# Moving steps between the slots of a scan: u one slot up, x_proj and softplus two slots apart, part of the MLP and the next norm behind softplus

## The chip, the cores and the metric

The kernel runs on one core of one Trainium2 chip. The metric is the device time of one execution in microseconds (us). Three runs of the kernel before gave 12441.65 us as the median, with 12438.44 and 12444.25 us at the ends.

## The reference

The network has four layers over an image `x` of 4 x 256 x 64 x 64 (batch, channels, rows, columns), each of the form `x = x + layer(groupnorm(x))`. Layers 0 and 1 are a gated recurrence followed by window attention. Layer 2 is a Mamba layer over the 4096 tokens of an image with 512 inner channels. Layer 3 is a grouped Mamba layer: the 256 channels are cut into 4 groups of 64, each group has 128 inner channels, and all groups share the weights. The change touches layers 2 and 3. Both have this core, and layer 3 has an MLP and an output convolution after it:

```
xi, z  = split(xn @ in_proj)                    # xn: layer norm of the tokens
u      = silu(causal_conv4(xi) + conv_b)
dt, B, C = split(u @ x_proj)
delta  = softplus(dt @ dt_proj + dt_b)
h_t    = exp(delta_t * A) * h_(t-1) + (delta_t * u_t) * B_t     # 16 states a channel
y      = (sum_n h_n * C_n + u * D) * silu(z)
layer 2:  out = y @ out_proj
layer 3:  m = layernorm(y @ out_proj)
          m = gelu(m @ fc1 + b1) @ fc2 + b2 + skip * xn
          out = silu(batchnorm(outc @ m))
```

## The kernel before

`net_kernel` loops over the 4 images of the batch and runs the attention layers, `mamba_layer` and `grouped_mamba_layer` on each. Nothing overlaps between images except at the edges, so the program is four nearly equal pieces.

**Slots.** Both Mamba layers hand a list of 16 blocks to `scan_blocks`: 4 chunks `k` of 1024 tokens by 4 blocks of 128 channels. A block has 16 slots, one for each state `n`. In layer 3 a block is one channel group; the four groups of a chunk form two pairs `c = 0, 1`, and a pair is an *even* block followed by an *odd* one. So the blocks of a chunk are even c=0, odd c=0, even c=1, odd c=1.

**What a slot issues.** The order is written out by hand (manual schedule), and each engine executes its instructions in that order. For slot `i`, `scan_blocks` issues, in this order: on VectorE (DVE) the product `pb = du * B` (L914) and the scan `h` (L920); on GpSimd (POOL) `product(i + 2)` (L830) and `hc = h * C` (L926); on ScalarE (ACT) `decay(i + 3)`, which is `da = exp(delta * A)` (L856), and `keep` of the last column (L861); the loads of C and B rows on the DMA queue; then the background steps of the slot, `blk["bg"]`; then on TensorE (PE) `spread(i + 2)`, which broadcasts a row of B into PSUM (L844), and `turn(i - 1)`, eight transposes that sum `hc` into `y` (L872); and last `decay(i + 2, True)` on ACT.

**Slots apart.** Slots 0, 4 and 8 of layer 3 (0, 5 and 10 of layer 2) are *apart*: their product with B is made on POOL from a loaded row (`bb`), so DVE has no L914 there and PE no spread. Their decay is the tile `dap`, written to PSUM, and it is issued at the end of the slot two before, behind that slot's background steps:

```
            for step in blk["bg"].get(n, ()):
                step()
            ...
            spread(i + 2)
            turn(i - 1)
            decay(i + 2, True)
```

**Buffers.** `da` has four buffers, `h` and `hc` three, the PSUM tiles `pb` and `dap` share two, and all other PSUM work of a layer shares two buffers of the tag `mm`.

**Background steps.** `put(block, slots, steps)` hangs steps on slots. The ones that the change moves are these.

- `all_u` / `in_u` (L1574, L1581): the four convolution taps as matmuls, four pieces of a pair; the first of two pieces takes both `mm` buffers, the second evicts them on ACT. `silu(.., "u")` (L1606) loads an activation table, takes Silu of the two tiles and loads the exp/ln table back (L950).
- `x_proj` (`table_steps`): two projections evicted on ACT (L1073), the second with the stores of B and C to DRAM; then a copy to bf16 on ACT (`part(P)`, L1081), a POOL difference (`rest(64)`, L1084), an ACT copy (`part(64)`) and a POOL difference (`rest(32)`), which give the three bf16 parts that spread reads.
- `delta` (`delta_steps`, "softplus"): `proj(s)` is a matmul and Abs, Exp, Ln on ACT (L1043 to L1045), `add(s)` is a DVE step (L1049), `times_u` a POOL product (L1053).
- `mlp`: `out_proj` (L1642, two ACT steps L1647 and L1648), `deviation` (L1652, then Ln and Exp), `scale` (POOL, L1657), `hidden(0)` (L1663), `fc1` (table load, Gelu, `hidden(1)` on PE, Gelu, table load; L1670), `fc2(0)`, `fc2(1)` (L1686, L1691, eviction L1696). `m0` and `m1` are the halves of the pair before.
- `norm` of the next chunk: `mean`, `center`, `deviation`, `scale`, `affine`; `h0` and `h1` are its halves. `out_conv` (L1711, L1717) is the output convolution, `out` (L1736) adds x on POOL and stores.

The product of `y` with `silu(z)` is two DVE steps of slot 3 (L886), which read the `mm` tiles `fin_ps` (L897) of slot 2.

Of the kernel before, what the change touches and what calls it, by code (L numbers as in the profile page):

```python
# [45 lines left out]
class Net:  # L46
# [1068 lines left out]
    def mamba_layer(self, x, bridge, pe_dram, w_in, w_cw, w_x, w_dt, w_out, v_dram):  # L1115
        tc, nc = self.tc, self.nc
        ND = 4
        with ExitStack() as ctx:
# [148 lines left out]
            def delta(k, d):  # L1267
                return self.delta_steps(
                    chunks[k]["blocks"][d], wdt[:, d * P : (d + 1) * P], work, psum
                )  # L1270
# [76 lines left out]
            for k in range(n_chunk):  # L1347
                more = k + 1 < n_chunk
                bg = [blk["bg"] for blk in chunks[k]["blocks"]]

                def put(d, where, steps):
                    for i, f in zip(where, steps):
                        bg[d].setdefault(i, []).append(f)

                if k == 0:
                    put(0, (2, 3, 4, 5), folds)
                if k:
                    for i, where in enumerate(((3, 4, 5), (6, 7, 8), (9, 10, 11), (12, 13, 14))):
                        put(0, where, out_proj(k - 1, i // 2, i % 2))
                put(0, (9, 10, 11, 12, 12), delta(k, 1))  # L1360
                put(0, (14, 15), (in_z(k, 0, 0), in_z(k, 0, 1)))
                put(1, (1,), (silu((k, 0, "zs")),))
                put(1, (6, 7, 8, 9, 10), delta(k, 2))
                put(1, (11, 12), (in_z(k, 1, 0), in_z(k, 1, 1)))
                put(1, (14,), (silu((k, 1, "zs")),))
                at = (6, 7, 8, 9, 10) if more else (5, 6, 7, 8, 9)
                put(2, at, delta(k, 3))
                at = (10, 11) if more else (8, 9)
                put(2, at, (in_z(k, 2, 0), in_z(k, 2, 1)))
                z3 = in_z(k, 3, 0), in_z(k, 3, 1)  # L1370
                if more:
                    put(3, (0, 1), z3)
                else:
                    put(2, (10, 11), z3)
                if more:

                    if k == 0:
                        put(0, (0,), (lambda: begin(1),))
                        put(0, (0, 0, 1, 3, 4, 5, 6, 7), self.later(lambda: norm(1, 0), 8))
                    h1 = self.later(lambda k=k: norm(k + 1, 1), 8)  # L1380
                    if k:
                        put(0, (2, 4, 5, 7, 8, 13, 14, 15), h1)
                    else:
                        put(0, (7, 8, 9, 12, 13, 14, 15), h1[:7])
                        put(1, (1,), h1[7:])
                    if k + 2 < n_chunk:
                        put(3, (3,), (lambda k=k: begin(k + 2),))
                        h0 = self.later(lambda k=k: norm(k + 2, 0), 8)
                        put(3, (4, 6, 7, 14, 15), h0[:5])
                        chunks[k + 1]["late"] = ((0, 1, 2), h0[5:])  # L1390
                    if k:
                        put(0, *chunks[k]["late"])
                    u = all_u(k + 1)
                    put(1, range(5, 16), u[:11])
                    put(2, range(14), u[11:25])
                    put(3, (1, 2, 3, 4, 5, 5, 6), u[25:])
                    xs = x_proj(k + 1)
                    put(2, (13,), (silu((k + 1, 0, "u"), (k + 1, 1, "u"), (k + 1, 2, "u"),
                                        (k, 2, "zs")),))
                    put(3, (7,), (silu((k + 1, 3, "u"), (k, 3, "zs")),))  # L1400
                    put(3, (7, 8, 8, 9, 9, 10, 11, 12), xs)
                    put(3, (9, 10, 10, 11, 12), delta(k + 1, 0))
                else:
                    put(2, (13,), (silu((k, 2, "zs"), (k, 3, "zs")),))

                    sums, about, square, squares, early_squares = stats

                    def square_into(i):
                        tag, bufs = ("pe", 1) if i % 2 else ("u", 5)
                        square(i, work.tile([P, NC], F32, tag=tag, name="cs_sq", bufs=bufs))  # L1410

                    for i in range(6):
                        put(1 + (13 + i) // DS, ((13 + i) % DS,), (lambda i=i: sums(i),))
                        put(2 + (12 + i) // DS, ((12 + i) % DS,), (lambda i=i: square_into(i),))
                        put(2 + (13 + i) // DS, ((13 + i) % DS,), (lambda i=i: squares(i),))
                    put(2, (3,), (about,))
                    put(3, (3,), (early_squares,))
                    for i in range(4):
                        at = (6 + 2 * i, 7 + 2 * i)
                        put(3, at, out_proj(k, i // 2, i % 2, ((0, 1, 2),)))  # L1420
# [70 lines left out]
    def grouped_mamba_layer(self, x, bridge, begun, ws_dram, outc_dram, v_dram, out_b):  # L1491
        tc, nc = self.tc, self.nc
        w_in, w_cw, w_x, w_dt, w_out, w_f1, w_f2 = ws_dram
        with ExitStack() as ctx:
# [113 lines left out]
            def silu(k, c, key, also=()):  # L1608
                def step():
                    for blk in chunks[k]["blocks"][2 * c : 2 * c + 2]:  # L1610
                        silu_of(blk, key)
                    for f in also:
                        f()
                    self.exp_ln_tables()

                return step
# [14 lines left out]
            def delta(k, q):  # L1631
                return self.delta_steps(chunks[k]["blocks"][q], wdt, work, psum)
# [108 lines left out]
            def all_u(k, c):  # L1741
                return [in_u(k, c, s, i) for s in range(2) for i in range(2)]
# [109 lines left out]
            for i, (k, c) in enumerate(pairs):  # L1852
                even, odd = chunks[k]["blocks"][2 * c : 2 * c + 2]

                def put(blk, where, steps):
                    for i, f in zip(where, steps):
                        blk["bg"].setdefault(i, []).append(f)


                for where, steps in late:  # L1860
                    put(even, where, steps)
                late = []
                more = c == 1 and k + 1 < n_chunk

                if more:
                    h0, h1 = (self.later(lambda k=k, s=s: norm(k + 1, s), 5) for s in range(2))
                    put(even, (0,), (lambda k=k: begin(k + 1),))
                    put(even, (0, 1, 4, 5, 6), h0)
                    put(even, (14, 15), h1)
                    put(odd, (1, 2, 3), h1[2:])  # L1870
                put(even, (4, 5, 6, 7, 8, 9), x_proj(k, 2 * c + 1))
                if i:
                    m0, m1 = mlp(*pairs[i - 1], 0), mlp(*pairs[i - 1], 1)
                    put(even, (5, 6, 7, 10, 11, 12, 13), m0)
                    put(even, (6, 7, 8), m1)
                    if c == 0:
                        put(even, (14, 15), m1[3:])
                        put(odd, (0, 1), m1[5:])
                    else:
                        put(odd, (15,), m1[3:])  # L1880
                        late.append(((0, 1, 1), m1[4:]))
                put(even, (7, 8, 8, 9, 10), delta(k, 2 * c + 1))
                also = [lambda k=k: out_silu(k - 1)] if c == 1 and k else []
                if i == 0:
                    put(even, (1, 2), [in_z(0, 0, s) for s in range(2)])
                    put(even, (1, 2), [lambda ss=ss: scale(1, ss, nc.gpsimd) for ss in first])
                    put(even, (3, 3), [lambda ss=ss: affine(1, ss) for ss in first])
                    also = [lambda blk=odd: silu_of(blk, "u")]
                put(even, (3,), (silu(k, c, "zs", also),))
                if c == 1 and k:  # L1890
                    put(even, (4, 4, 5, 5), [out(k - 1, *sm) for sm in outs])
                if c == 0 and k:
                    put(odd, (10, 12, 15), [out_conv(k - 1, *sm) for sm in outs[:3]])
                    late.append(((0,), [out_conv(k - 1, *outs[3])]))

                if i + 1 < len(pairs):
                    nk, ncol = pairs[i + 1]
                    put(odd, (4, 5, 6, 7), all_u(nk, ncol))
                    put(odd, (7,), (silu(nk, ncol, "u"),))
                    put(odd, (8, 8, 8, 9, 10, 11), x_proj(nk, 2 * ncol))  # L1900
                    put(odd, (9, 10, 10, 11, 12), delta(nk, 2 * ncol))
                    put(odd, (13, 14), [in_z(nk, ncol, s) for s in range(2)])
            self.scan_blocks(
                [blk for c in chunks for blk in c["blocks"]], loop, psum, psb, psy, (0, 4, 8),
# [125 lines left out]
```

## Time and profile before

| what | us |
|---|---|
| median of three runs | 12441.65 |
| profiled execution, its own time | 12439.35 |
| span of the profiled execution | 12437.6 |
| DVE busy | 10216.3 (82%) |
| PE busy | 10255.9 (82%) |
| POOL busy | 9018.9 (73%) |
| ACT busy | 7245.9 (58%) |
| scans of layer 2, image 1 (4188.1 to 5141.5) | 953.40 |
| scans of layer 3, image 1 (5195.7 to 6162.7) | 967.00 |
| scans of layer 3, images 0, 2, 3 | 968.50, 967.10, 969.10 |

All times are us from the span's start. The line numbers are those of the kernel before. An engine's busy time counts its own instructions; idle time in front of an instruction is put down to the instruction that released it. The time of an execution is 1.75 us longer than its span.

### The profile page before, as it was taken

How to read it: one execution, taken by the hardware profiler on the slowest of the kernel's cores; microseconds unless marked ns; L12 is line 12 of the kernel's file. 1: busy time of each engine (PE TensorE's matmuls, PEld its weight loads, DVE VectorE, ACT ScalarE, POOL GpSimd, SP SyncE). 2: the span in 40 equal slices, each digit the busy share in tenths (PEclk: the TensorE clock that was granted, in tenths of full speed). 3: DMA queues.
4: the chain of work that ended last, by engine and by line, in shares of the span. 5: the costliest groups of instructions: out<-in, count | busy, mean ns of one | idle time of the engine just before them, and what ended most of it. 6: DMA issues, size and time to landing. Idle time of an engine off the chain costs nothing. (4 is left out here: it accounts for less than half of the span.)

```text
span 12437.6 us, 159552 instructions
## 1 busy us (share of the span) xinstructions
PE 10255.9 (82%) x54592; PEld 6015.9 (48%) x54592; DVE 10216.3 (82%) x9130; ACT 7245.9 (58%) x13300; POOL 9018.9 (73%) x4634
## 2 busy tenths in 40 slices
PE   8987887787898788777789878877878987887777
PEld 4664544443466454444346645444434664544443
DVE  6777898897677799889767779988976777998897
ACT  4565554776466555477645655547754565554775
POOL 4666886887466688688746668868874666886887
PEclk9999998999899999899889999989988999998998
DMA  3343554454334455454433434545543343554454
GB/s 96 108 128 131 168 169 147 167 169 142 97 108 127 132 169 170 146 168 167 144 95 109 127 130 172 169 146 167 169 142 95 109 127 130 172 170 146 167 170 140
DMA packets 680299, 1773.54 MB, mean 143 GB/s; under 512 B 89120, under 2 KB 195120, under 8 KB 678464
## 3 DMA queue, kind: packets, MB, share of 16 engines
q1 hardware_dynamic: 679488, 1763.34, 43.7%
q8 instruction: 435, 7.13, 0.2%
q14 instruction: 376, 3.08, 0.1%
HBM read 1601.51 MB, written 94.37 MB: 136 GB/s over the span
## 5 line engine op out<-in xcount | busy, mean ns | idle before, releaser
L926 POOL TENSOR_TENSOR hc<-h,cb 128x1024 f32<-128x1024 f32 x2056 | 4814.1, 2350 | 988.2 <-DVE h L920 425.6
L920 DVE TENSOR_TENSOR_SCAN h<-da,m_state,pb 128x1024 f32<-128x1024 f32 x1248 | 2919.9, 2340 | 161.7 <-DVE pb L914 2.8
L872 PE MATMUL y<-ident,hc 128*128 128x128 f32 x16384 | 2371.0, 293 | 346.7 <-POOL hc L926 259.0
L872 PEld LDWEIGHTS y<-ident,hc 128*128 128x128 f32 x16384 | 2091.8, 152 | 1009.7 <-POOL hc L926 439.0
L914 DVE TENSOR_TENSOR pb<-du,pb 128x1024 f32<-128x1024 f32 x1672 | 2024.8, 1211 | 92.5 <-PE pb L844 89.3
L856 ACT ACTIVATE da<-delta,m_v 128x1024 f32<-128x1024 f32 x1672 | 1898.8, 1141 | 220.8 <-DVE h L920 204.0
L844 PE MATMUL pb<-m_parts,pick 128*128 128x512 bf16 x3312 | 1099.8, 417 | 872.2 <-DVE h L920 821.8
L502 ACT ACTIVATE pr<-sc,mn 128x256 f32<-128x256 f32 x2048 | 956.6, 478 | 770.8 <-PE pt_ps L528 551.2
L514 POOL TENSOR_TENSOR pr<-pr,sm 128x1024 f32<-128x1024 f32 x512 | 967.9, 1897 | 560.0 <-DVE sm L512 380.6
L844 PEld LDWEIGHTS <-pick 128*128 128x128 bf16 x3312 | 255.2, 101 | 1883.1 <-DVE h L920 1160.3
L920 DVE TENSOR_TENSOR_SCAN h<-da,pb 128x1024 f32<-128x1024 f32 x424 | 969.6, 2287 | 55.6 <-DVE pb L914 1.4
L830 POOL TENSOR_TENSOR bb<-du,bb 128x1024 f32<-128x1024 f32 x376 | 888.8, 2364 | 65.2 <-DMA bb<-m_cd 60.5
L491 DVE TENSOR_REDUCE mn<-sc 128x4 f32<-128x1024 f32 x512 | 609.6, 1219 | 244.9 <-PE sc L480 242.8
L920 DVE TENSOR_TENSOR_SCAN h<-dap,m_state,bb 128x1024 f32<-128x1024 f32 x288 | 672.0, 2333 | 76.2 <-ACT dap L856 63.4
L528 PE MATMUL pt_ps<-ident,pr 128*128 128x128 f32 x4096 | 571.6, 283 | 145.7 <-ACT pts L541 64.3
L208 PE MATMUL conv_ps<-att_y,att_wb 128*128 128x512 f32 x1536 | 688.8, 593 | 0.0
L856 ACT ACTIVATE dap<-delta,m_v 128x1024 f32<-128x1024 f32 x376 | 419.6, 1116 | 422.3 <-DVE h L920 298.2
L552 PE MATMUL ov_ps<-pts,kv 128*64 128x128 f32 x8192 | 583.6, 289 | 91.6 <-DVE vimg L565 75.6
L480 PE MATMUL sc<-kv,q 64*128 64x128 f32 x8192 | 573.0, 288 | 81.7 <-DMA kv<-kv_dram 68.0
L528 PEld LDWEIGHTS pt_ps<-ident,pr 128*128 128x128 f32 x4096 | 465.8, 144 | 315.4 <-issue 151.4
L480 PEld LDWEIGHTS sc<-kv,q 64*128 64x128 f32 x8192 | 515.8, 196 | 124.3 <-issue 56.1
L552 PEld LDWEIGHTS ov_ps<-pts,kv 128*64 128x64 f32 x8192 | 456.4, 141 | 217.2 <-DVE vimg L565 131.9
(270 smaller groups left out, 18063.0 us busy)
## 6 DMA issues: line engine op xcount, KB each, us to landing
cb<-m_cd SPq DMA_DIRECT2D x2048, 512.0 KB
kv<-kv_dram SPq DMA_DIRECT2D x2048, 128.0 KB
bb<-m_cd SPq DMA_DIRECT2D x376, 512.0 KB
q<-q SPq DMA_DIRECT2D x256, 256.0 KB
kv_dram<-kst SPq DMA_DIRECT2D x128, 256.0 KB
kv_dram<-vn SPq DMA_DIRECT2D x128, 256.0 KB
x<-in_x_dram SPq DMA_DIRECT2D x8, 2048.0 KB
m_pe<-in_pe_dram SPq DMA_DIRECT2D x32, 512.0 KB
```

The lines of the kernel that those rows point to most:

```text
L480: nc.tensor.matmul(sc[w][:, r, cq, :], qbuf[sj % 2][m][rows, b, 2 * a + w].rearrange("p h t -> p (h t)"), t[rows, :, k0 : k0 + 64], start= ...
L502: nc.scalar.activation(t[:, cq].rearrange("p j r t -> p r j t"), sc[w][:, :, cq, :].rearrange("p r (j t) -> p r j t", j=2), AF.Exp, bias=m ...
L514: nc.gpsimd.tensor_tensor(t, t, s.rearrange("p (a o) -> p a o", o=1).to_broadcast([P, 4, 256]), ALU.mult,)
L528: nc.tensor.transpose(pt[w][j][:, cq, :], t[:, cq, j].rearrange("p r t -> p (r t)"), self.ident,)
L552: nc.tensor.matmul(ov[i][b * 64 : b * 64 + 64, m, :, :, w, :], t[:, j, c0 : c0 + 64], pts[w][j][:, cq, :], start=(j == 0), stop=(j == 1),)
L830: nc.gpsimd.tensor_tensor(pb[i], slots[i][0]["du"], pb[i], ALU.mult)
L844: nc.tensor.matmul(pb[i][:, ss], self.pick[:, n : n + 1].to_broadcast([P, P]), blk["parts"][:, ss], start=True, stop=True,)
L856: nc.scalar.activation(da[i], blk["delta"], AF.Exp, scale=blk["a"](n))
L872: nc.tensor.matmul(blk["y"][:, ss], t[:, ss], self.ident, is_transpose=True, start=(n == 0 and ss.start % NT == 0), stop=(n == DS - 1 and ...
L914: nc.vector.tensor_tensor(pb[i], blk["du"], pb[i], ALU.mult)
L920: nc.vector.tensor_tensor_scan(h[i][:, ss], da[i][:, ss], pb[i][:, ss], state, ALU.mult, ALU.add)
L926: nc.gpsimd.tensor_tensor(hc[i][:, ss], h[i][:, ss], cb[i][:, ss], ALU.mult)
```

## The change

Only `put` calls are changed; every step stays, and no tile or buffer count changes. In layer 2, x_proj's projections and softplus of block 3 are put two slots apart and the bf16 splitting follows softplus. In layer 3, odd blocks issue u and its Silu one slot earlier (3 to 6), x_proj's projections at 8 and 9, softplus from 10 and the splitting at 10 to 13, and the output convolution at 13 to 15. Even blocks issue the projections at 4 and 5, softplus from 7 (c=0) or 8 (c=1), the splitting at 10 to 13, the first steps of `m1` behind softplus, `m0` one slot later for c=1, and the rest of `h0` at 13 to 15.

```diff
@@ mamba_layer
-                    put(3, (7, 8, 8, 9, 9, 10, 11, 12), xs)
-                    put(3, (9, 10, 10, 11, 12), delta(k + 1, 0))
+                    put(3, (7, 8, 8, 9), xs)
+                    put(3, (10, 11, 11, 12, 12), delta(k + 1, 0))
+                    put(3, (10, 11, 12, 13), xs[4:])
@@ grouped_mamba_layer
                 if more:
                     ...
-                    put(even, (0, 1, 4, 5, 6), h0)
+                    put(even, (0, 1, 13, 14, 15), h0)
                     put(even, (14, 15), h1)
                     put(odd, (1, 2, 3), h1[2:])
-                put(even, (4, 5, 6, 7, 8, 9), x_proj(k, 2 * c + 1))
+                xs, ds = x_proj(k, 2 * c + 1), delta(k, 2 * c + 1)
+                put(even, (4, 5), xs)
+                put(even, (8, 9, 9, 10, 10) if c else (7, 8, 8, 9, 9), ds)
+                put(even, (10, 11, 12, 13), xs[2:])
                 if i:
                     m0, m1 = mlp(*pairs[i - 1], 0), mlp(*pairs[i - 1], 1)
-                    put(even, (5, 6, 7, 10, 11, 12, 13), m0)
-                    put(even, (6, 7, 8), m1)
+                    put(even, (10, 11, 12) if c else (9, 10, 11), m1)
+                    put(even, (6, 7, 8, 11, 12, 13, 13) if c else (5, 6, 7, 10, 11, 12, 13), m0)
                     ...
-                put(even, (7, 8, 8, 9, 10), delta(k, 2 * c + 1))
                 ...
                 if c == 0 and k:
-                    put(odd, (10, 12, 15), [out_conv(k - 1, *sm) for sm in outs[:3]])
+                    put(odd, (13, 14, 15), [out_conv(k - 1, *sm) for sm in outs[:3]])
                     ...
                 if i + 1 < len(pairs):
                     nk, ncol = pairs[i + 1]
-                    put(odd, (4, 5, 6, 7), all_u(nk, ncol))
-                    put(odd, (7,), (silu(nk, ncol, "u"),))
-                    put(odd, (8, 8, 8, 9, 10, 11), x_proj(nk, 2 * ncol))
-                    put(odd, (9, 10, 10, 11, 12), delta(nk, 2 * ncol))
+                    put(odd, (3, 4, 5, 6), all_u(nk, ncol))
+                    put(odd, (6,), (silu(nk, ncol, "u"),))
+                    xs = x_proj(nk, 2 * ncol)
+                    put(odd, (8, 9), xs)
+                    put(odd, (10, 11, 11, 12, 12), delta(nk, 2 * ncol))
+                    put(odd, (10, 11, 12, 13), xs[2:])
                     put(odd, (13, 14), [in_z(nk, ncol, s) for s in range(2)])
```

## The prediction

> **What bounds the kernel now.** I first read the stages by windows, since the change touches only the Mamba layers: layer 3's scans take about 967 us of each image, and DVE is busy for 873 of them.
>
> ```profile
> core 0: us, PE busy (x) PEld busy (x) DVE busy (x) ACT busy (x) POOL busy (x), PEclk, DMA share, GB/s
> 5195.70:6162.70 967.00, 741.24 (x3474) 410.98 (x3472) 873.21 (x531) 658.40 (x952) 852.84 (x387) 0.90 0.50 169
> ```
>
> So DVE sets the pace, and what can be won or lost in this layer is its idle time. POOL, at 853 us, has little room. Next I read who DVE waits for in the same window (us in total, times, longest):
>
> ```profile
> DVE delta L1049 <- ACT delta L1045: 33.7, 20, 2.6
> DVE pb L914 <- PE pb L844: 15.3, 13, 4.5
> DVE h L920 <- ACT dap L856: 12.3, 4, 4.2
> DVE h L920 <- POOL bb L830: 1.3, 1, 1.3
> ```
>
> The other images give 34.0, 33.6 and 33.8 us for the first line and 13.1, 12.9 and 12.6 for the third. The first line is softplus: `add(s)` waits for Abs, Exp and Ln of its half. Taken block by block it is 17.6 us in the seven odd blocks, 5.9 in the even c=0 and 10.1 in the even c=1 blocks. The third line is the even c=1 blocks alone.
>
> The timeline of ACT in an odd block (k=1, c=0) shows why softplus is late. Scan 6 starts at 5520.93, scan 7 at 5524.54, scan 8 at 5526.80, and scan 10 at 5533.98:
>
> ```profile
> 5521.28 1.15 ACT L856 ACTIVATE da<-delta,m_v 128x1024 f32<-128x1024 f32 x1
> ...
> 5523.32 1.12 ACT L856 ACTIVATE dap<-delta,m_v 128x1024 f32<-128x1024 f32 x1 [0.80 <-DVE h L920]
> ...
> 5526.39 1.27 ACT L1581 ACTIVATE m_u<-u_ps,m_v 128x512 f32<-128x512 f32 x2 [0.79 <-PE u_ps L1574]
> 5527.68 1.28 ACT L1606 ACT_TABLE_LOAD   x1
> 5528.97 2.00 ACT L1606 ACTIVATE m_u<-m_u 128x1024 f32<-128x1024 f32 x2
> 5530.98 1.28 ACT L950 ACT_TABLE_LOAD   x1
> ```
>
> Evictions, two loads and two Silu hold ACT from 5526.39 to 5532.26, 5.87 us, and all that follows is late until add(0) has waited 2.41 us. But `dap`, the decay of apart slot 8, stands ahead of this stretch, because Silu is in slot 7 and `dap` was issued at the end of slot 6. PE decides when the stretch can start:
>
> ```profile
> 5514.77 1.99 PE L1574 MATMUL u_ps<-m_xn,m_wi 64*128 64x512 f32 x8
> ...
> 5518.10 1.99 PE L1574 MATMUL u_ps<-m_xn,m_wi 64*128 64x512 f32 x8
> ...
> 5521.43 1.99 PE L1574 MATMUL u_ps<-m_xn,m_wi 64*128 64x512 f32 x8
> ...
> 5524.38 1.99 PE L1574 MATMUL u_ps<-m_xn,m_wi 64*128 64x512 f32 x8
> ```
>
> A piece of u with the spread and the transposes behind it takes 3.33 us of a slot of 3.60: here PE runs without a pause.
>
> **Odd blocks.** Softplus moves to slots 10 to 12, two slots behind x_proj, when ACT has caught up: its waits, 17.6 us an image, go. The Silu moves to slot 6, and the order of instructions puts it ahead of `dap` of slot 8. The wait added is DVE's scan 8 on `dap`; behind `dap` on ACT stand the decays of slots 10 and 11, and behind scan 8 hc of slot 8 on POOL and spread(10) on PE, none of which is late by itself. Its length: the first piece, now in slot 3, needs both `mm` buffers, which the slot's two products by silu(z) release at 5513.8 (DVE rows 5512.55, 1.26 long). That is 1.0 us before the old start, not 3.6, since PE had no pause to fill. Three periods of 3.33 later the fourth piece starts at 5523.8 and ends at 5525.8. ACT then needs 5.87 us and `dap` 1.12, with 0.1 for hand-over: 5532.9. Scan 8 could start 2.26 after scan 7. Scan 7 slips by 0.35, because spread(5) now stands behind the first piece (5513.8 + 2.0 + 0.5 = 5516.3 against 5515.99), so it could start at 5527.15. The wait is 5.8. New per image: 7 x (5.8 + 0.35) = 43.1; removed 17.6; together +25.5. Bounds of the wait: 3.6, if the slot-6 piece ran where the old slot-6 piece ran (ends 5523.4), and 6.6, if u were no earlier at all and PE 0.4 later, as it is in the c=1 blocks. I take 5.8 as it follows from consecutive rows.
>
> The Trainium skill, "ScalarE: Activation LUTs", section "Table sets: the hidden batching unit", charges about 2.7 us for each switch of table set, and another passage of that page gives 1283 ns. The rows here show 1.28 us, and the measurement decides. By the larger figure the stretch would be 2.8 us longer and the sum some 80 us higher, an estimate from that page (2.8 x 7 x 4).
>
> **Even c=0.** x_proj keeps 4 and 5, the bf16 copy and the halves of m1 (out_proj and deviation, 3.5 us of ACT with the copy) leave slots 6 and 7, so add(0) no longer waits: -5.9. What comes into slots 10 to 12 stands in front of or behind Gelu, where in this block (k=1) ACT waited 2.36 us for scan 10 just ahead of Gelu, so I cost it at nothing; were that cover gone, hidden(1) would delay spread(13), as in the next part.
>
> **Even c=1.** The norm's deviation and affine, the copy and m1 leave slots 4 to 7; the row of before shows what they did:
>
> ```profile
> 5591.05 2.35 DVE L920 TENSOR_TENSOR_SCAN h<-dap,m_state,bb 128x1024 f32<-128x1024 f32 x1 [4.25 <-ACT dap L856]
> ```
>
> The removed waits are 10.1 (delta), 12.3 (dap) and 1.3 (bb): 23.7. New ones are these. (a) POOL still has four `out` sums of 1.25 in slots 4 and 5, and product(8) behind them: 1.3, what the block without a norm (k=3) already waits; three blocks, 3.9. (b) softplus's matmul stands behind the transposes of that late POOL: 0.5, three blocks, 1.5. (c) Now the ACT copy `part(64)` stands in slot 12 ahead of Gelu, and it needs `rest(64)` on POOL. From the end of scan 10, POOL does hc 2.35, du 2.35, then hc from 4.7 to 7.0 and rest(64) to 9.2; the copy ends at 10.2, the table load at 11.5, the first Gelu at 12.1, hidden(1) (1.7) and spread(14) (0.6) at 14.5. Scan 13 ends at 0.69 + 1.21 + 2.35 + 2 x 3.60 = 11.45. DVE waits 3.1, in four blocks: 12.4. (d) In slot 13 PE then has transposes 0.9, the norm's deviation 2.6, fc2(0) 1.9, fc2(1) 1.05 and spread(15) 0.5: at 21.3, against scan 14's end at 14.5 + 1.21 + 2.35 = 18.05. That is 3.3 for three blocks and 0.7 for k=3, 10.6. New: 28.4, net +4.7. Bounds: the two long waits could vanish (-23) if POOL is early; 10 more if they add to each other. I take the chain, whose rows are all here.
>
> **Block changes.** rest(64), du, rest(32) and product(0) of the next block now stand in slots 11 to 14 in a row: with three hc and at 2.31 or 2.09 us from start to start, product(0) ends 15.8 after scan 11's end; DVE gets there after 2 x 4.25 (with add) + 2 x 3.56 = 15.6, so 0.25 x 7. hc of slot 14 is then 2.3 later, the transposes wait for it, and with out_conv and the norm's mean (1.7 each) in slot 0 spread(2) of the c=1 blocks comes 1.1 late, twice. Together +4.0 (0 to 8). The stores of B and C move from slot 8 to slot 9 on the DMA queue; the first load that reads them (bb) is in slot 12, so I cost that at nothing; without those three slots POOL's product(0) would wait for the row, and DVE for POOL. in_z with out_conv in slots 13 and 14 is 2.7 us of PE, inside the slot.
>
> **Layer 2.** Waits for softplus in image 1 are 7.7 us in 4, of which block 3 has 7.0 in three. They go; the later rest(64) can cost POOL up to 1.0 at the next block. -6.0 (-7.7 to 0).
>
> **Sum.** Per image +25.5 - 5.9 + 4.7 + 4.0 - 6.0 = +22.3; four images +89. The profiled execution took 12439.35 us (span 12437.6), so 12528; the median of the runs stands 2.3 higher, 12441.65, so 12531.
>
> **Rivals.**
> *Silu is in time* (faster). If `dap` of slot 8 comes less than 2.6 us late, the change wins: without the odd waits the sum is -5.9 + 4.7 + 4.0 - 6.0 = -3.2, and 17.6 - 2.5 + 3.2 = 18.3 is 7 x 2.6. If that wait is hidden altogether and (c) and (d) too, each image saves 17.6 + 5.9 + (23.7 - 5.4) + 6.0 - 4.0 = 43.8 and the time is 12266. For it: DVE has these waits to give, and ACT is busy for only 658 of 967 us. Against it: from the start of scan 6 scan 8 can follow after 5.86 us, and in that time ACT would have to do 5.87 + 1.12 us, behind a piece of u on PE.
> *It cancels* (no change). PE reaches the slot-6 piece by 5521.4: the wait is 3.6, there is no wait at spread(5), and the sum is 7 x 3.6 - 17.6 - 5.9 + 4.7 + 4.0 - 6.0 = +4.4 an image, 12459. Against it: that is a piece before PE's rows allow. That u is not really a slot earlier is part of my forecast.
> *It costs more* (slower). With 6.6 in the odd blocks and 10 more in the even c=1 blocks and 4 at block changes, +42 an image: 12610. POOL's 853 of 967 us speaks for it; that DVE's new waits let POOL catch up speaks against it.
>
> **How the numbers follow.** Forecast 0.62, silu in time 0.13, cancels 0.12, costs more 0.13. A measurement of this kernel can tell about 0.2%, 25 us, from no change. Faster 0.13; same 0.08, most of the third case; slower 0.79. The range is 12425 to 12610: below it stand the first rival's times, above it a little of the last. Its lower end is the cancelling case with (c) and (d) half as long (4.4 - 11.5 = -7 an image, 12413) drawn in a little, its upper end the last rival.
>
> **What would show it.** Right: the line of DVE waiting for L1045 falls from 33.7 to under 5, and DVE waiting for `dap` rises from 12.3 to about 40 an image, seven waits of 5 to 6 us in the odd blocks at slot 8; L914 waiting for L844 rises from 15 to about 40. Wrong: `dap` waits under 3 us in odd blocks (then it is faster), or no wait at slots 13 and 14 of the even c=1 blocks.

## The result, and the profile after

The changed kernel takes 12628.95 us (median of four runs, 12616.83 to 12630.0); the kernel before takes 12442.95 (median of four). The ratio is 1.0149, 95% interval 1.0134 to 1.0164: 186 us slower, where 89 were forecast. The sign held, the forecast had half the size, and the time lies above its range.

By stages of the profiled executions (spans 12628.2 and 12437.6): layer 3's scans add up to 4074.2 us over the four images instead of 3871.7 (+202.5; forecast +113), layer 2's to 3793.1 instead of 3818.8 (-25.7; forecast -24). The remaining +13.8 lies in the phases between, which the edit does not touch and which vary by 19 us over the runs below. Five runs of one kernel below lie 33 us apart, so single runs are judged by their sum over layer 3's scans; two profiles of that kernel differ by 2.7 us in it. The row by windows for the same image as before:

```profile
5238.30:6257.00 1018.70, 766.45 (x3472) 426.02 (x3472) 874.87 (x531) 659.29 (x952) 852.95 (x387) 0.88 0.48 160
```

No engine has more to do: DVE, ACT and POOL are busy within 2 us of what they were, and PE, with no more matmuls than before, is busy 25 us longer at a lower mean clock (0.88 of full speed, 0.90 before). Some 50 of the 51.7 us more are idle time of DVE. The waits of DVE in that window (us in total, times, longest):

```profile
DVE pb L914 <- PE pb L844: 51.7, 31, 4.8
DVE h L920 <- ACT dap L856: 46.3, 11, 5.8
DVE delta L1049 <- ACT delta L1045: 7.9, 5, 2.4
DVE h L920 <- POOL bb L830: 6.5, 8, 1.3
```

Softplus fell from 33.7 to 7.9 (under 5 forecast), as the change wants. Its place was taken by `dap` (12.3 before, about 40 forecast) and by the spread L844 (15.3 before, about 40 forecast). ACT's timeline in the odd block that the prediction worked on (k=1, c=0; L1582 evicts u, L1607 is Silu) shows the first:

```profile
5579.61 1.26 ACT L1582 ACTIVATE m_u<-u_ps,m_v 128x512 f32<-128x512 f32 x2 [4.18 <-PE u_ps L1575]
5580.89 1.28 ACT L1607 ACT_TABLE_LOAD   x1
5582.18 2.01 ACT L1607 ACTIVATE m_u<-m_u 128x1024 f32<-128x1024 f32 x2
5584.21 1.28 ACT L950 ACT_TABLE_LOAD   x1
5585.50 1.12 ACT L856 ACTIVATE dap<-delta,m_v 128x1024 f32<-128x1024 f32 x1
```

The decay of apart slot 8 stands behind the whole Silu stretch, and ACT had been idle for 4.18 us waiting for the fourth piece of u on PE. DVE's row there:

```profile
5586.72 2.35 DVE L920 TENSOR_TENSOR_SCAN h<-dap,m_state,bb 128x1024 f32<-128x1024 f32 x1 [5.65 <-ACT dap L856]
```

The forecast was 5.8. What the forecast did not have is in PE's timeline of the even c=1 block (k=1, image 1):

```profile
5649.97 1.97 PE L872 MATMUL y<-ident,hc 128*128 128x128 f32 x8 [2.93 <-POOL hc L926]
5651.86 2.07 PE L1041 MATMUL dt_ps<-m_bct,m_wdt 64*128 64x512 f32 x2
...
5656.19 1.12 PE L1041 MATMUL dt_ps<-m_bct,m_wdt 64*128 64x512 f32 x2
...
5657.69 1.04 PE L872 MATMUL y<-ident,hc 128*128 128x128 f32 x8
...
5672.58 2.65 PE L1664 MATMUL f_ps<-m_sq,m_wf 64*128 64x512 f32 x4 [5.96 <-ACT hid L1671]
5675.16 1.04 PE L844 MATMUL pb<-m_parts,pick 128*128 128x512 bf16 x2
```

The same eight transposes take 1.97 us after an idle stretch and 1.04 a little later, the same matmul of softplus 2.07 and 1.12. hidden(1), which the prediction priced at 1.7, takes 2.65, and the spread behind it 1.04 instead of 0.6. The windows of that block say why; the column before the DMA share is the granted clock, the share of full speed that PE is given:

```profile
5650.00:5656.00 6.00, 6.00 (x20) 3.69 (x20) 3.53 (x3) 1.96 (x4) 6.00 (x4) 0.52 0.58 184
5656.00:5670.00 14.00, 9.93 (x45) 4.55 (x43) 13.53 (x10) 9.94 (x17) 11.75 (x6) 0.98 0.45 135
5670.00:5676.00 6.00, 3.42 (x7) 1.37 (x8) 1.58 (x1) 4.37 (x7) 6.00 (x4) 0.50 0.55 204
```

After PE has idled it works at half clock for several us, and those are just the matmuls that someone waits for.

### The profile page after: what moved, and what is told of

It is laid out like the page before. It is cut to its first block, busy times and chain, and to the rows that moved or that the text cites. A ratio compares the mean times of both kernels' runs of the same rounds, so it can differ in the third digit from the quotient of the medians.

```text
span 12628.2 us, 159616 instructions
## 1 busy us (share of the span) xinstructions
PE 10328.7 (82%) x54592; PEld 6060.3 (48%) x54592; DVE 10221.3 (81%) x9130; ACT 7249.0 (57%) x13300; POOL 9023.5 (71%) x4634
## 5 line engine op out<-in xcount | busy, mean ns | idle before, releaser
L844 PE MATMUL pb<-m_parts,pick 128*128 128x512 bf16 x3312 | 1089.7, 414 | 1036.5 <-DVE h L920 964.2
L844 PEld LDWEIGHTS <-pick 128*128 128x128 bf16 x3312 | 255.9, 100 | 2100.9 <-DVE h L920 1055.6
```

The source lines that it names most:

```text
L844: nc.tensor.matmul(pb[i][:, ss], self.pick[:, n : n + 1].to_broadcast([P, P]), blk["parts"][:, ss], start=True, stop=True,)
```

## The experiments

The sum over layer 3's scans in the four images is 4074.2 us in the changed kernel and 3871.7 in the kernel before. "Per image" is a quarter of a difference of such sums; waits are means over images 1 to 3 or of image 1. A wait of slot n lies behind scan n, ahead of DVE's next instruction; only the odd blocks' waits for `dap` "of slot 8" are named by the scan that waits.

### 1. u and its Silu back (odd blocks)

```diff
-put(odd, (3, 4, 5, 6), all_u(nk, ncol))
-put(odd, (6,), (silu(nk, ncol, "u"),))
+put(odd, (4, 5, 6, 7), all_u(nk, ncol))
+put(odd, (7,), (silu(nk, ncol, "u"),))
```

> The changed kernel with the four pieces of u back in odd slots 4 to 7 and their Silu back in slot 7; x_proj and softplus stay two slots apart. My theory: the odd blocks' 39.9 us of waits of scan 8 for `dap` come from the Silu stretch standing ahead of that `dap` on ACT. They go to 0 with nothing in their place, because add(0) comes only in slot 11, by when Abs, Exp and Ln have caught up; the .35 us wait of spread(5) goes too. Layer 3 falls by about 42 us an image, from 1018.5 to about 976, and the run by about 170 us, to some 12460. Rival (ACT is simply behind by that much and DVE pays at softplus instead): `dap` waits go but waits for Ln of 2 to 2.7 us come back in each odd block; layer 3 falls by only 22 to 25 us an image and the run by about 95.

Layer 3's sum is 3926.6, 36.9 per image less, and the run 12478.54. DVE's waits in image 1:

```profile
DVE delta L1049 <- ACT delta L1045: 7.8, 5, 2.4
...
DVE h L920 <- ACT dap L856: 6.2, 4, 2.4
```

`dap` goes from 46.3 to 6.2 (none of it is at slot 8), and softplus does not come back. So softplus two slots later costs the odd blocks nothing; moving u and Silu a slot up cost them 37 us an image. ACT's rows show the order that did it:

```profile
5526.79 1.12 ACT L856 ACTIVATE dap<-delta,m_v 128x1024 f32<-128x1024 f32 x1 [1.12 <-DVE h L920]
...
5529.57 1.27 ACT L1582 ACTIVATE m_u<-u_ps,m_v 128x512 f32<-128x512 f32 x2 [0.50 <-PE u_ps L1575]
```

Of the 42 expected 5 are missing: waits for PE grew elsewhere, among them 2.5 us at slot 9 of the image's first odd block and 1.0 at the norm's centering behind it.

### 2. Only the Silu back

```diff
-put(odd, (6,), (silu(nk, ncol, "u"),))
+put(odd, (7,), (silu(nk, ncol, "u"),))
```

> The changed kernel with the Silu of u alone back in odd slot 7; the pieces of u stay in slots 3 to 6. My theory (the order on ACT, Silu ahead of `dap` of slot 8, makes the wait): the `dap` waits fall from 39.9 us an image to under 3, though u's pieces stay where they are; the .35 us wait of spread(5) stays in each odd block (2.5 an image). Layer 3 about 979 us an image, the run about 160 us shorter than the changed kernel. Rival (the earlier place of u's pieces on PE, and of their evictions on ACT, makes it): the `dap` waits stay at over 3 us a block and the run falls by less than 60 us.

Sum 3940.1, 33.5 per image less; run 12485.94. The wait of odd slot 8 falls from 5.65 to about 1.0 in each block, 7 us an image and not under 3: `dap` now stands behind one eviction of u that itself waits for PE. The order on ACT makes 4.7 of the 5.7 us, the place of u's pieces the rest.

### 3. Gelu ahead of part(64) (even c=1)

```diff
-put(even, (10, 11, 12, 13), xs[2:])          # ahead of the MLP's steps
+if not (c and i): put(even, (10, 11, 12, 13), xs[2:])
 ...                                          # m1, m0
+if c: put(even, (10, 11, 12, 13), xs[2:])
```

> The changed kernel with the bf16 splitting of even c=1 blocks issued behind the MLP in slots 10 to 13, so that Gelu comes ahead of the copy part(64) on ACT in slot 12. My theory, step (c): scan 13's waits for its spread, 18.0 us an image in four blocks, come from Gelu standing behind part(64), which waits for rest(64) on POOL. They fall to under 4 us an image, those of slot 14 (12.3) by some 4 as well; layer 3 falls by 15 to 20 us an image, the run by 60 to 80. Rival (Gelu is late from ACT's other work or PE's, the splitting only stands in a pause): under 4 us an image less.

Sum 4006.5, 16.9 per image less; run 12553.04. Slot 13's waits, 18.0 us an image, fall to 0.4. In the changed kernel ACT's rows for that slot were

```profile
5669.47 1.06 ACT L1081 ACTIVATE m_parts<-m_bct 64x1024 bf16<-64x1024 f32 x1 [3.64 <-POOL m_bct L1084]
5670.54 1.28 ACT L1671 ACT_TABLE_LOAD   x1
5671.84 1.27 ACT L1671 ACTIVATE hid<-f_ps,m_f1b 128x512 f32<-128x512 f32 x2
```

and with Gelu first

```profile
5644.03 1.26 ACT L1671 ACTIVATE hid<-f_ps,m_f1b 128x512 f32<-128x512 f32 x2
...
5648.51 1.06 ACT L1081 ACTIVATE m_parts<-m_bct 64x1024 bf16<-64x1024 f32 x1
```

Step (c) is shown: ACT stood 3.64 us behind a copy that waited for POOL, with Gelu ready behind it. Slot 14's waits fell from 12.3 to 8.6.

### 4 and 5. PE kept busy until Gelu

```diff
+put(even, (12,) * 3, [again] * 3)     # again = hidden(0), the same values; 3 and then 6 times, c=1
```

> The changed kernel with hidden(0) of the MLP repeated three times on PE in slot 12 of the even c=1 blocks, ahead of hidden(1): the repeats write the values that are there already, and only add PE work (some 5 to 7 us in each of 16 blocks) where PE was waiting. Theory of the clock: PE comes out of its wait of 5.96 us at a granted clock of 0.50, so that hidden(1) takes 2.65 us and the spread behind it 1.04 instead of some 1.7 and 0.60. With PE kept busy until then hidden(1) takes 1.7 to 1.9, and scan 13's wait falls from 4.3-4.8 to about 3.1-3.5 in each block (by about 5 us an image), though PE has more to do. Rival (the wait is ACT's and POOL's chain alone and the clock is of no account): scan 13's wait stays or grows.

> As the kernel with three repeats of hidden(0) in slot 12 of the even c=1 blocks, but with six. With three, PE ended the repeats 3.03 us before Gelu released hidden(1); hidden(1) began at full clock and was at half clock after 0.7 us, so it still took 2.65 us. Six take about 2.9 us more and end just before. Theory of the clock: hidden(1) takes 1.7 to 1.9 us and the spread behind it 0.60, and scan 13's wait falls by 1.2 to 1.4 us in each of the four blocks against the changed kernel's 4.17 to 4.81. Rival (clock of no account): scan 13's wait stays or grows.

Three repeats: sum 4058.7, 3.9 per image less, run 12615.91. Six: 4036.9, 9.3 less, run 12589.09. PE's rows with three and with six (k=1 of image 1; hidden is L1665 and Gelu L1672 in these kernels):

```profile
5668.44 2.65 PE L1665 MATMUL f_ps<-m_sq,m_wf 64*128 64x512 f32 x4 [3.03 <-ACT hid L1672]
```

```profile
5653.55 5.42 PE L1665 MATMUL f_ps<-m_sq,m_wf 64*128 64x512 f32 x24
5659.74 1.70 PE L1665 MATMUL f_ps<-m_sq,m_wf 64*128 64x512 f32 x4 [0.77 <-ACT hid L1672]
5661.38 0.60 PE L844 MATMUL pb<-m_parts,pick 128*128 128x512 bf16 x2
```

Idle for 5.96 or 3.03 us before it, hidden(1) takes 2.65; idle for 0.77, it takes 1.70, and the spread 0.60. With three repeats the blocks of image 1 differ among themselves, which tells the two theories apart. In k=1 hidden(1) still takes 2.65, and the wait of slot 13 stays (4.64 us, 4.65 in the changed kernel). In k=2, where PE was idle for only 1.43 us, it takes 1.70, and the wait falls from 4.17 to 2.79:

```profile
5928.48 1.70 PE L1665 MATMUL f_ps<-m_sq,m_wf 64*128 64x512 f32 x4 [1.43 <-ACT hid L1672]
...
5930.76 1.23 DVE L914 TENSOR_TENSOR pb<-du,pb 128x1024 f32<-128x1024 f32 x1 [2.79 <-PE f_ps L1665]
```

So some 1.4 us of each wait of slot 13 was the clock, and more work for PE made the kernel faster. With six repeats hidden(1) takes 1.70 in every even c=1 block, but slot 13's waits fell only from 18.0 to 15.4 us an image, where a fall of 5 was expected: Gelu, which reads what the repeats write, now waits for their end, 2.6 us an image in all. ACT's row in the block above:

```profile
5659.00 1.27 ACT L1672 ACTIVATE hid<-f_ps,m_f1b 128x512 f32<-128x512 f32 x2 [0.39 <-PE f_ps L1665]
```

Slot 14's waits fell from 12.3 to 9.5; where the rest of the 9.3 comes from was not tried.

### 6. out_conv back to slots 10, 12, 15

```diff
-put(odd, (13, 14, 15), [out_conv(k - 1, *sm) for sm in outs[:3]])
+put(odd, (10, 12, 15), [out_conv(k - 1, *sm) for sm in outs[:3]])
```

> The changed kernel with out_conv back in odd slots 10, 12 and 15. My theory: the odd c=0 blocks' waits of slot 15 for `dap` (2.42, 1.18 and 2.45 us in the three blocks that have out_conv) come from ACT evicting two out_conv and two z ahead of that `dap` in slots 13 and 14; with out_conv spread out they go to under 0.4 each. Layer 3 about 6 us an image shorter, the run about 20 to 24. Rival (the splitting's rest(32) and product(0) on POOL make the end of the odd block late): the waits stay at over 1 us, or turn into waits for POOL's bb of the same length.

The waits for `dap` at the end of the three blocks went, from 2.42, 1.18 and 2.45 to waits for POOL of 0.2 to 0.3 us. Nothing was won where 6 us an image were expected: the sum is 4078.9, 1.2 per image more, and the run 12632.82. DVE's rows (the block's first scan, and the norm's centering in the next slot) and a PE row between them:

```profile
5616.06 2.35 DVE L920 TENSOR_TENSOR_SCAN h<-dap,m_state,bb 128x1024 f32<-128x1024 f32 x1 [0.18 <-POOL bb L830]
...
5624.61 1.22 DVE L980 TENSOR_TENSOR m_xn<-x,ln_pm 128x1024 f32<-128x1024 f32 x1 [2.59 <-PE ln_pm L977]
```

```profile
5620.14 2.71 PE L1712 MATMUL oc_ps<-xo,m_woc 128*128 128x512 f32 x4
```

The 2.4 us came back a slot later as 2.6. POOL's rest(32), product(0) and hc set when PE may do its transposes; PE idles till then, and out_conv (1.88 at full clock, 2.71 here) and the norm's mean stand behind them. By these rows POOL had caught up while DVE stood still at the old wait: there were two late chains of nearly one length, and the edit took one.

### 7. Even c=1 blocks as before

```diff
-put(even, (0, 1, 13, 14, 15), h0)
+put(even, (0, 1, 4, 5, 6), h0)
 ...                                  # c=1 alone: x_proj 4 to 9, m0 from 5, m1 6 to 8, softplus 7 to 10
```

> The changed kernel with the even c=1 blocks as before (norm's deviation and affine in 4 to 6, x_proj and the splitting in 4 to 9, m0 from 5, m1 in 6 to 8, softplus in 7 to 10); all else as changed. From first scan to last these four blocks take 274.9 us an image in the changed kernel and took 254.1 before. My theory after the result: the whole 20.8 belongs to this edit, four times what the prediction gave it (+4.7), so layer 3 falls by about 21 us an image and the run by about 83. Rival: the prediction's sum was right and the rest of the 20.8 comes into these blocks from the odd blocks ahead of them (POOL late); then the run falls by some 20 us only, and the four blocks stay at over 265 us.

Sum 4003.7, 17.6 per image less; run 12543.48. The four blocks take 253.7 us again instead of 274.9, so their loss is their own edit's: 21 where the prediction had 4.7. The other blocks took 3.6 back.

### 8 and 9. Two local waits taken away

The `out` sums on POOL spread out, and (on top of experiment 3) fc2 later:

```diff
-put(even, (4, 4, 5, 5), [out(k - 1, *sm) for sm in outs])
+put(even, (4, 5, 6, 9), [out(k - 1, *sm) for sm in outs])
```

```diff
-put(even, (6, 7, 8, 11, 12, 13, 13) if c else (5, 6, 7, 10, 11, 12, 13), m0)
+put(even, (6, 7, 8, 11, 12, 14, 15) if c else (5, 6, 7, 10, 11, 12, 13), m0)
```

> The changed kernel with the four `out` sums of the even c=1 blocks on POOL in slots 4, 5, 6 and 9 instead of 4, 4, 5, 5; nothing else. Theory: product(8) behind four sums on POOL is the 1.28 us wait of slot 7, and the late POOL leaves PE idle for 2.9 us, so that transposes and softplus's matmul run at half clock, which makes slot 9's wait of 2.33 us. Both go in three blocks: slot 7 to 0, slot 9 to under 0.6; layer 3 about 9 us an image shorter, the run about 36. Rival (slot 9's wait is ACT, behind out_proj and the norm's tables, and POOL's lateness is unimportant for it): slot 7's wait goes and slot 9's stays, layer 3 about 4 us shorter.

> As the kernel with Gelu ahead of part(64), and fc2 of m0 in even c=1 slots 14 and 15 instead of both in 13. Theory, step (d): slot 14's waits, 1.70, 3.58, 3.16 and 0 us in that kernel, come from PE doing the norm's deviation and both fc2 ahead of spread(15); they fall to under 1 us each, with at most half a us more in slot 15. Layer 3 falls by 5 to 7 us an image against that kernel, the run by 20 to 28. Rival (PE is simply full at the end of the block): the waits move to slot 15 and the next block's slot 0, and layer 3 falls by under 2 us.

Spread out, slot 7's waits of 1.28 went and slot 9's of 2.33 fell to 0, 0.6 and 1.0 (k=1, 2, 3), as the theory has it: the late POOL made them. But the sum fell only to 4057.0, 4.3 per image where 9 were expected. DVE came earlier to a Gelu that is still late, because POOL, now at work without a pause and with an `out` sum in slot 9, ends rest(64) no earlier; in block k=1 of image 1 slot 13's wait grew from 4.65 to

```profile
5662.99 1.23 DVE L914 TENSOR_TENSOR pb<-du,pb 128x1024 f32<-128x1024 f32 x1 [6.27 <-PE pb L844]
```

With fc2 later, slot 14's waits (1.70, 3.58, 3.16 and 0) fell to under 0.8 in all blocks but one (1.25), and the sum stayed: 4007.0 against experiment 3's 4006.5. The waits came back in slots 1 to 3 of the block behind, mostly for PE: the rival, two slots later than it had it. Run 12540.83.

### 10, 11 and 12. Mended, and what the c=1 move is then worth

All of experiments 1, 3, 6, 8 and 9 together, with the splitting in the odd blocks in slots 9 to 12, first once and then in rounds:

> Everything found so far mended in the changed kernel: u and its Silu back in odd 4 to 7, Gelu ahead of part(64) in the even c=1 blocks, out_conv back in odd 10, 12, 15, and three moves more: the four `out` sums on POOL in even slots 4, 5, 6 and 9 instead of 4, 4, 5, 5 (so that product(8) is not late), fc2 in even c=1 slots 14 and 15 instead of both in 13, and the splitting in the odd blocks in slots 9 to 12 instead of 10 to 13. My theory, term by term an image against the changed kernel: odd blocks -40, Gelu -18, out_conv -6, `out` -3.9 and half of slot 9's 7 us, fc2 -6: layer 3 falls from 1018 to 940 to 945 us, and the run to 12310 to 12350, under the kernel before. Rival (POOL and PE have no room, so that what is pushed out of one place comes back in another): the sum is not met, layer 3 stays above 960 and the run above 12400.

> The mended kernel again, timed in five rounds. One run gave 12345.92 us beside 12436.03 for the kernel before. My theory: the gain is real, 12335 to 12360 us and a ratio of 0.992 to 0.994. Rival: the attention phases, which the edits don't touch and which vary by some 10 us from run to run, made part of it, and the ratio is 0.996 or more.

One run gave 12345.92; five gave a median of 12334.42 beside 12433.51 for the kernel before, ratio 0.992, interval 0.9906 to 0.9933. It is faster than both kernels: 99 us under the kernel before, 295 under the changed one. Layer 3's sum is 3789.8, 947 an image where 940 to 945 were expected (71.1 per image under the changed kernel, where the single edits add up to 36.9 + 16.9 + 4.3 - 1.2 - 0.1 = 56.8; the splitting's earlier place was not run alone), layer 2's keeps its gain. DVE's waits in image 1:

```profile
DVE pb L914 <- PE pb L844: 14.4, 10, 4.3
DVE m_zs L886 <- PE fin_ps L897: 10.7, 9, 2.4
...
DVE delta L1049 <- ACT delta L1045: 5.8, 9, 1.2
...
DVE h L920 <- ACT dap L856: 0.7, 1, 0.7
```

Softplus (33.7 in the kernel before) is down to 5.8 and `dap` (12.3) to 0.7 together; the line that grew (from 4.2) is `fin_ps` behind PE at the head of the odd c=1 blocks, where experiment 9's waits had gone. The same with the even c=1 blocks as before the change:

> The mended kernel with the even c=1 blocks as before the change (with the odd blocks, even c=0 and layer 2 of the mended one). Tells what the move behind softplus in those blocks is worth once Gelu, `out` and fc2 are mended: the four blocks take 241.5 us an image in the mended kernel and 254.1 before. My theory: they are what tells the two apart, so this one is 4 x 12.6 = 50 us slower than the mended kernel, at about 12396, still under the kernel before. Rival (the blocks' gain is paid back in the odd blocks behind them, whose first slots wait longer in the mended kernel): the difference is under 20 us.

12372.62 us, ratio 0.9951 (0.9936 to 0.9966): 38 us behind the mended kernel, where 50 were expected. The four blocks are 16.5 us an image longer (256.6 against 240.1) and the odd c=1 blocks behind them 10.0 shorter (224.9 against 234.9). So the move of the MLP and the norm behind softplus is worth something once its queues are in order, but about half of the blocks' gain is paid back next door (10.0 of 16.5; by the other profile of the mended kernel 7.1 of 15.0): part of the rival held. The rest of the 38 us is in other blocks and phases.

## Why the prediction was right or wrong

The direction, the odd blocks and layer 2 were right. Two steps failed. One is a price: in even c=1 the prediction put PE's work behind a wait, (b) and (c), at rows of full clock, and it came at half clock, 1.9 us more in three blocks and 1.4 more in four, 11.3 us an image. The other is a path: the queues at a block's end, which it put at nothing in even c=0 and "inside the slot" at the block changes.

**Odd blocks: right.** Seven waits of slot 8 came to 39.9 us an image (forecast 40.6), those of spread(5) to 2.6 (2.5), and softplus's 17.6 went. Experiment 1 puts the cause where the text did, Silu ahead of `dap` on ACT; experiment 2 adds that u's place on PE makes 1 of the 5.7 us.

**Layer 2: right,** -25.7 against -24 in all.

**Even c=1, (a) and the removed waits: right.** 1.28 in three blocks; of the 23.7 all but 0.6 went. That 0.6 is a reading that was off: one wait of the `dap` line lies in an even c=0 block, and it stayed.

**Even c=1, (b) mis-sized.** "softplus's matmul stands behind the transposes of that late POOL: 0.5": it was 2.33 to 2.36 in the three blocks, with smaller waits beside it 8.2 us an image instead of 1.5. Transposes and matmul took 1.97 + 2.07 where full clock gives 1.04 + 1.12, so by these rows 1.9 of each wait is PE's clock after an idle stretch of 2.93 us. Experiment 8 removes POOL's lateness, and with it the slow clock; it shows the cause, but not how much of the wait is the clock's.

**Even c=1, (c) mis-sized.** The chain was right to a tenth as far as Gelu: rest(64) ended 9.2 us after scan 10 (forecast 9.2), the copy 10.3 (10.2), the first Gelu 12.3 (12.1). Then "hidden(1) (1.7) and spread(14) (0.6)" took 3.6 instead of 2.3, and the wait was 4.2 to 4.8 instead of 3.1: 18.0 us an image instead of 12.4. The six repeats give 1.70 and 0.60 back. The trace of before had both prices. There hidden(1) took 2.04 to 2.24 in six of the sixteen even c=1 blocks, at a mean granted clock of 0.73 to 0.81, as in k=0 of image 1; the prediction took k=1:

```profile
5362.37 2.04 PE L1663 MATMUL f_ps<-m_sq,m_wf 64*128 64x512 f32 x4 [1.79 <-ACT hid L1670]
5364.34 1.03 PE L844 MATMUL pb<-m_parts,pick 128*128 128x512 bf16 x2
...
5607.35 1.70 PE L1663 MATMUL f_ps<-m_sq,m_wf 64*128 64x512 f32 x4 [1.79 <-ACT hid L1670]
5608.99 0.71 PE L844 MATMUL pb<-m_parts,pick 128*128 128x512 bf16 x2
```

**Even c=1, (d): about right,** 12.3 instead of 10.6 (the terms that it lists add up to 21.45, not 21.3, 0.5 us an image).

**Even c=0: wrong.** The four blocks became 0.9 us longer, not 5.9 shorter. Softplus's wait did go. New are 1.9 us an image in slots 12 and 13, behind the Gelu of which it said "so I cost it at nothing", and 4.1 in slots 1 and 2. There hidden(1) of the late half MLP in slots 0 and 1 stands on PE behind transposes that wait for POOL, which now has rest(32) ahead of product(0): in block k=2 the transposes began 2.3 us after the block's first scan (5751.19), 1.3 before (5682.81). The rows of before and after:

```profile
5684.10 1.67 PE L872 MATMUL y<-ident,hc 128*128 128x128 f32 x8 [0.54 <-POOL hc L926]
```

```profile
5753.52 1.97 PE L872 MATMUL y<-ident,hc 128*128 128x128 f32 x8 [1.97 <-POOL hc L926]
```

No run tried POOL's order there by itself. This is "hc of slot 14 is then 2.3 later", which the prediction followed into the c=1 blocks and not into these.

**Block changes: wrong.** "in_z with out_conv in slots 13 and 14 is 2.7 us of PE, inside the slot": PE got to it late, ACT evicts two out_conv and four z after it, and the next block's `dap` stands behind them on ACT. ACT's rows at the end of the odd c=0 block of k=1, and DVE's first scan behind it:

```profile
5615.19 0.60 ACT L1602 ACTIVATE m_zs<-z_ps 128x512 f32<-128x512 f32 x1 [0.27 <-PE z_ps L1597]
5616.13 0.60 ACT L1602 ACTIVATE m_zs<-z_ps 128x512 f32<-128x512 f32 x1 [0.34 <-PE z_ps L1597]
5616.63 1.11 ACT L856 ACTIVATE dap<-delta,m_v 128x1024 f32<-128x1024 f32 x1
...
5617.84 2.35 DVE L920 TENSOR_TENSOR_SCAN h<-dap,m_state,bb 128x1024 f32<-128x1024 f32 x1 [2.42 <-ACT dap L856]
```

With POOL's share the ends of the odd blocks cost 8.2 us an image. That is the fault that the prediction had worked out for slot 8 and did not look for here. Experiment 6 shows that it would have been paid anyway, by PE.

In all, even c=1 took 16.1 us an image more than forecast, even c=0 6.8 and the odd blocks 3.5, less 4.0 booked as block changes: 22.4, which is what was missed ((202.5 - 113) / 4). Of the 16.1, (b) makes 6.7, (c) 5.6 and (d) 1.7. "Costs more" was the rival nearest to it, for another reason than the one it gave.

The range failed because its upper end summed the same rows, all at full clock; with (b) at 2.4 and (c) at 4.5 the forecast would have been 12531 + 4 x 11.3 = 12576, inside the range and still 53 short.

On the clock, the Trainium skill, "TensorE: Matmul & The Clock Gate", Part 1, names two states, 4/8 and 8/8, and says that the array falls to the lower one after about one idle window of some 3.4 us. The records of this case agree on the two levels, 0.50 and 1.00, but no length of idle divides them. In layer 3's scans of the changed kernel the first microsecond of PE's work ran at half clock behind 65 of 68 idle stretches of 3 us or more, behind 42 of 110 of 2 to 3 us (2.93 in the rows above), and behind 18 of 216 of 1 to 2 us. The same page, "Why this matters for your kernels", warns against idle gaps of over some 3 us between matmul bursts; that speaks straight to this change, and it was not weighed: the change opens gaps of 2.9 and 6.0 us on PE ahead of work that DVE waits for.

## What to carry to other kernels

When a step is moved up, list what stands behind it in each in-order queue, and ask first for the item with a deadline: the copy, the Silu or the eviction costs nothing itself and delays a decay that does. Price PE's work behind a wait of three us or more at half clock, up to twice its full-clock row, and look for work to put into that gap. Read a price from all blocks of a trace and not from one. And a wait that is taken away is a gain only if the next late chain is shorter by as much: two of five local mends here moved their whole gain to the next slot or block, and only together did the mends beat the kernel before.

## What the hardware did that was not expected

PE's granted clock was 0.50 or 1.00 and nothing between (other figures above are means over a stretch). It fell in idle stretches of 2.9 to 6.0 us (0.50 to 0.52 in the windows above), and for some 4 to 6 us the work after them took up to twice as long: 1.97 for 1.04 us of transposes, 2.65 for 1.70 us of fc1. Every half-clock stretch within layer 3's scans, before and after, lasted 3.41 us or a whole multiple of it. Six repeats of hidden(0), 5.4 us of PE work that changes no value in each of 16 blocks, took 37 us off layer 3's scans (4036.9 against 4074.2; the run 12589.09 against 12628.95) with nothing else changed.
